# A planned order of work made anew: expert weight loads planned beside SyncE, other planned lengths for z's loads, stores and scatters

## The chip, the core and the metric

The kernel runs on one core of one Trainium2 chip. The core has a matrix engine (TensorE, here PE), a vector engine (VectorE, DVE), a scalar engine (ScalarE, ACT), a general engine (GpSimd, POOL) and an engine that issues DMA transfers (SyncE, SP). Each runs its own queue of instructions in order and meets the others through semaphores. The metric is the device time of one execution in microseconds; 876.67 us before the change (median of 3 runs, 876.44 to 877.49).

## What is computed

Four layers in a row, each followed by a residual add and a layernorm (float32, 8 sequences of 512 tokens, 256 features):

```python
x = _layernorm(x + _L0_attn_ref(x, ...))   # retention, 16 heads
x = _layernorm(x + _L0_ffn_ref(x, ...))    # ternary weights, GELU, layernorm inside
x = _layernorm(x + _L1_attn_ref(x, ...))   # per-token linear attention over the heads
x = _layernorm(x + _L1_ffn_ref(x, ...))    # mixture of experts, below
```

The change is mostly about the last layer. Tokens form two groups of 2048. Each group's tokens pick two of 8 experts (a capacity of 160 rows per expert and group); an expert is two matmuls with weights of 1 MB each, and its output, times the gate, is added back to the token's row:

```python
expert_in = jnp.einsum('gtec,gth->egch', dispatch, x)
h = jax.nn.relu(jnp.einsum('egch,ehf->egcf', expert_in, wi))
expert_out = jnp.einsum('egcf,efh->egch', h, wo)
y = jnp.einsum('gtec,egch->gth', combine, expert_out)
```

## The kernel before

The kernel is a set of streams of stages: per half or whole sequence `a0`, `a1`, `a2` (retention), `b`, `bn` (the ternary feed-forward), `c1`, `hd`, `ca`, `c2` (the second attention), then choosing and routing (`t`), loading expert weights (`w`, `load_expert`, line 1760), gathering rows (`g`, `gather`), transposing them (`d`), the two expert matmuls (`h`, `e`), adding back (`s`, `combine`, line 1904) and the last layernorm (`f`, `finish`, line 2071). Each stage is a Python generator.

No order stands in the code as such. While the kernel is built, a planner keeps a clock: `op` (line 204) books an instruction on an engine for a planned length (its `cost`) at the first gap after its inputs' planned times, and puts it into a heap by planned start; `flush` (line 277) emits instructions in that order. So planned times decide three things: the order of instructions in every engine's queue, which engine takes a copy (`either` picks the one that would be through first), and where PE gets fillers. They insert no wait: at run time an instruction waits for semaphores of its true dependencies, and behind what stands ahead of it in its queue.

`interleave` (line 343) takes the string `turns` (line 2189), one letter for each turn of a PE stage; the next turn goes to the first stage in the string that can open. Where the next stage opens more than 1.4 us of planned time after PE's planned clock, it emits fillers, matmuls on a constant into an unused bank (`spare`, line 403), one for each 0.44 us. A filler has no reader.

SP issues all plain transfers through `dma` (line 703): `cost` is the time that the planner keeps SP's line, 0.4 us where nothing else is said, plus 1.9 us until the data is there (`LAND`). An expert's two weight loads are planned with cost 5.0 each (2.5 for a half), so while a 1 MB load is under way no other transfer may stand on SP's planned line.

The expert layer in order: group 0 takes experts 0 to 7, group 1 experts 7 to 0. They are numbered 0 to 15 in that order. Three are kept in memory for both groups (8, 9 and 10 use the weights of 7, 6 and 5); 11 and 12 use other buffers; 13, 14 and 15 are loaded into the three slots that 8, 9 and 10 free (`wi_13`, `wo_13` and so on). The output of a pair of experts is `eoT`, 320 rows transposed; PE turns it back in three parts (`eo_tp`, line 1921), DVE or ACT multiplies it by the gate (`eo_g_c`, group and column c, three columns for a pair), and POOL adds it to the rows of y in DRAM by an indirect transfer (here a scatter). Scatters of a group write the same tensor, so each waits for the landing of the one before. `combine` plans that by `Plan.landed`: 2.5 us after the scatter's issue, or near the end of a weight load that SP's line shows at that time.

When a group's scatters have landed, `finish` loads y for a sequence (`z_b`, 512 KB, cost 2.4), makes its layernorm (statistics on DVE, a power on POOL, the product on DVE for group 0 and on ACT for group 1) and stores it (cost 2.0). z_0 to z_3 belong to group 0 and run beside group 1's experts; z_4 to z_7 come at the end. The last pair of experts is not scattered: its outputs are summed on PE (`tail_ps`) and go straight to the output rows, after all stores. The copy of the last `eoT` from the matmul's bank is on DVE.

Of the kernel before, what the change touches and what calls it, by code (L numbers as in the profile page):

```python
# [21 lines left out]
B, S, D = 8, 512, 256  # L22
# [6 lines left out]
G = 2  # L29
# [54 lines left out]
def tile_layers(ctx: ExitStack, tc: tile.TileContext, ins, out, at):  # L84
    nc = tc.nc
# [38 lines left out]
    y_d = [dram.tile([TG + P, D], F32, name=f"y_d{g}") for g in range(G)]  # L124
# [16 lines left out]
    ACT, DVE, POOL, SP, GELU, EXP, DVS, POOLD = range(8)  # L141
# [5 lines left out]
    LAND = 1.9  # L147
# [8 lines left out]
    class Plan:  # L156
        now = 0.0
        slow = 0.0
        t = 0.0
# [4 lines left out]
        loaded = None  # L164
        shared = None, -9.0
        landed = 0.0
        free = {
            k: [(0.0, i) for i in range(n)] for k, n in dict(
                m4=M4, aq=AQ, x=XB, T=TB, b8=B8, w=EW, xsT=2, eoT=2, hT=2, ex=EX, scm=SCM, qz=2,
# [516 lines left out]
    with ExitStack() as stages:  # L686
# [16 lines left out]
        def dma(t, out, in_, cost=0.4):  # L703

            return op(SP, cost, t, nc.sync.dma_start, out=out, in_=in_) + LAND

        def rows_x(b):
            return x_d[b].rearrange("(c p) d -> p c d", p=P)
# [1051 lines left out]
        def load_expert(i):  # L1760
            _, e = order[i]
            kept = i - 2 * (i - E) - 1 if i >= E else None
            t = Plan.t
            if kept is not None and kept >= E - EW:
                weights[i] = weights[kept]
            else:
                if i == spare_w[0]:
                    held = [slot_tile(wk, "b8", [P, 2, FF], f"w_{i}_{j}") for j in range(2)]
                    parts = [w[:, j] for w in held for j in range(2)]
                elif i == spare_w[1]:  # L1770
                    held = [
                        slot_tile(wk, tag, [P, FF], f"w_{i}_{tag}_{j}") for tag in ("T", "hh")
                        for j in range(2)
                    ]
                    parts = list(held)
                else:
                    held = claimed("w")[1]
                    pool = pools[0 if held < 2 else 1]
                    wi = pool.tile([P, NK, FF], F32, tag=f"wi{held}", bufs=1, name=f"wi_{i}")
                    wo = pool.tile([P, NK, FF], F32, tag=f"wo{held}", bufs=1, name=f"wo_{i}")  # L1780
                    parts = [w[:, j] for w in (wi, wo) for j in range(2)]
                from_wi = ins["L1_ffn_wi"][e].rearrange("(k p) f -> p k f", p=P)
                from_wo = ins["L1_ffn_wo"][e].rearrange("(j f p) d -> p j f d", p=P, j=2)
                if i in spare_w[1:]:
                    for j in range(2):
                        t = max(t, dma(Plan.t, parts[j], from_wi[:, j], cost=2.5))
                    for j in range(2):
                        to = parts[2 + j].rearrange("p (f d) -> p f d", d=D)
                        t = max(t, dma(Plan.t, to, from_wo[:, j], cost=2.5))
                else:  # L1790
                    whole = held if i == spare_w[0] else (wi, wo)
                    t = max(t, dma(Plan.t, whole[0], from_wi, cost=5.0))
                    to = whole[1].rearrange("p j (f d) -> p j f d", d=D)
                    to, got = (v.rearrange("p j f d -> p (j f) d") for v in (to, from_wo))
                    t = max(t, dma(Plan.t, to, got, cost=5.0))
                parts[2:] = [w.rearrange("p (f d) -> p f d", d=D) for w in parts[2:]]
                weights[i] = parts, held
            yield later(t)
            return t
# [104 lines left out]
        def combine(i):  # L1904


            g, e = order[i]
            last = i >= len(order) - 2
            pair, half = divmod(e, 2)
            n_in = added[g, pair]  # L1910
            for j in ((0, 1), (1, 2))[half]:
                n_in[j] += 1
            for j, n in enumerate(COLS):
                if n_in[j] != (1, 2, 1)[j]:
                    continue
                n_in[j] = -9
                col = pair * 3 + j
                yield from need(0.0)
                ps = bank("eo_tp")
                for m in range(NK):  # L1920
                    T.transpose(
                        ps[:n, m * P : (m + 1) * P], eoT[g, pair][:, m, j * P : j * P + n], ident
                    )
# [15 lines left out]
                Plan.landed = done + 2.5  # L1939
                for a, b in Plan.busy[SP]:  # L1940
                    if b - a > 2.2 and a < done + 1.5 and b > done:
                        Plan.landed = max(Plan.landed, b - 0.5)
                give(eo, Plan.landed)
            if max(n_in) < 0:
                give(xsT[g, pair], Plan.now)
                give(eoT[g, pair], Plan.now)
            yield later(done)
            return done + (0.0 if last else 2.9)
# [122 lines left out]
        def finish(b):  # L2071

            g = b * G // B
            z = slot_tile(wk, "x", [P, NC, D], f"z_{b}")
            t = Plan.t
            landing = dma(t, z, rows_of(y_d, b), cost=2.4)
            landing = max(landing, t + (9.0 if g == 0 else 4.0 + 2.9 * (b - B // G)))
            yield later(landing)
            while b > B - 3 and "shown" not in tail:
                yield later(Plan.t + 0.3)  # L2080
            if b > B - 3:
                landing = max(landing, tail["shown"])
            e = max(layernorm(wk, z, z, [landing] * NC, on_act=(g == 1)))

            def store():
                stored.append(
                    nc.sync.dma_start(out=out[b].rearrange("(c p) d -> p c d", p=P), in_=z)
                )

            e = op(SP, 2.0, e, store)  # L2090
            tail["stored"] = max(tail.get("stored", 0.0), e + 0.5)
            give(z, e + 2.0)
            yield later(e + 2.0)
            return e + 0.5

        def after(*keys):
# [90 lines left out]
            ],  # L2187
        }
        turns = (
            "llnnnnlbbbbbhbbelbnbleceeeebleeeeleebcbblellbbelbelllcllbcnclerebbblbeeebellelcnnnnl"  # L2190
            "nnbclnbnbnclnbcbrcbrnllbnlbllnnhhblnncllhhhhblnnclbbbcnnhnbhcbncnnblbbjnjlllnbnlbjln"
            "jjbbbjjbbcjbhlnjjhlnhjhhhljhlnjbhnhllnblffcfnnnjjcflllnjcjjnnbclblfljnbjbllnbjlbcjbj"
            "nnllbbnlcjnffcjnnnbclllhffchbbnnnnlhllnnnnflhlbbbnlbnblfflhfflhbbbnlljhhhflffblbllfl"
            "lfnlnnlcffnfjnjjjfhbbnncnbfjnjhcfnjjfhnnnlhhhjjncjcjnfbbhhhnbnbfllbjlhlnhlhnffnnflhh"
            "hjnfnjnncfhjcjjcnnjlnffchcjjnfhllfjlnnjnnjjfffnffnnlhnjhjhhhhhhfffhjjjnnnnfcfcncjjfn"
            "nffnccfnnfnhnffjjnnnjjnjfjfjhhhhnjjnhnhjnjhhjffofjmffnnnnfhjjfffjnnjjoffjffoohfhooho"
            "hhhjjoohjojjfffhjrfmfmffffjfffjjmfrqqrfjmjrmqjmrqmmrrqrqqjjjmfmffqfjfjffffrmqqjqjqrf"
            "fqfqfqfpqqqpqrrpprprqrrfrqfqfffqppffffqrpqrrrfqfqfrrffrprqqpqqzpqqqpmoprrrroomrmpmmo"
            "mromropomqoooqmqrrprqrqrqqqqqqqqqprprrrpqprrppqqrpqpqqqrpqqqqqprrqqqqqqqqqqqqqqqqqpq"
            "mrrppqprrmrrpppmrrrrrpprrqprpyzzzzppp"  # L2200
        )

        interleave(
# [33 lines left out]
```

## Time and profile before

| | |
|---|---|
| median of 3 runs | 876.67 us |
| the profiled execution | 876.54 us |
| its span, first to last instruction | 874.8 us |
| mean granted PE clock | 0.987 |
| DVE, ACT, POOL busy | 616.6, 516.2, 328.6 us |
| DVE busy from 600 to 650 us | 46.9 of 50 |
| transfers | 106.89 MB, 122 GB/s on the mean |
| SP's queue of transfers | 42.0% of the 16 engines' span |
| POOL's queue of transfers | 3.5% |
| weight loads wi, wo | 11 and 11 of 1024 KB, and one more expert in parts |
| z loads and stores | 8 and 8 of 512 KB |

The page gives busy time of each engine, then groups of instructions by line. Nearly all instructions but PE's carry line 233, where the planner stores them, so groups are told apart by their tiles (`eo`, `z`, `spare`). A line of a timeline has the start, the length, the engine, the line and the operation, and in brackets how long the engine had been idle and what ended it. Matmuls in float32 run as two passes, and a timeline counts passes.

### The profile page before, as it was taken

The page shows a single profiled execution, that of the slowest core. Times are in us where ns is not written, and L with a number is a line of the kernel's source. Part 1 is how long each engine was busy: PE and PEld are TensorE (multiplying, and loading weights), DVE is VectorE, ACT ScalarE, POOL GpSimd, SP SyncE. Part 2 cuts the span into 40 slices and gives each one's busy share as a digit, 9 for nine tenths or more (in the row PEclk, how much of TensorE's full clock was granted, in tenths as well). Part 3 has the DMA queues.
Part 4 walks back from the last instruction along what each step waited for, and adds up shares of the span by engine and source line. Part 5 has one row for each costly group of instructions (what it writes and reads, how often), then busy time and mean ns, then how long its engine had stood idle before and what let it go on. Part 6 is the DMA issues. An engine that isn't in the chain of part 4 may idle for free. (4 is left out here: it accounts for less than half of the span.)

```text
span 874.8 us, 20560 instructions
## 1 busy us (share of the span) xinstructions
PE 829.8 (95%) x8128; PEld 682.0 (78%) x8128; DVE 616.6 (70%) x1669; ACT 516.2 (59%) x1047; POOL 328.6 (38%) x346
## 2 busy tenths in 40 slices
PE   7998999999999999999999999999999999999983
PEld 5877877986878887688778768768578889889971
DVE  4946678587898888677878888899986553713324
ACT  2436568648673777568788597676755463222223
POOL 1222462352344442244353524425253231372433
PEclk9999999999999999999999999999999999999995
DMA  7153111652722033622515607566587195649553
GB/s 215 25 171 114 44 37 25 121 161 36 174 66 62 18 74 58 168 70 39 115 59 98 170 26 147 192 143 147 173 165 231 46 307 157 209 120 331 139 127 111
DMA packets 201615, 106.89 MB, mean 122 GB/s; under 512 B 124432, under 2 KB 192208, under 8 KB 201328
## 3 DMA queue, kind: packets, MB, share of 16 engines
q1 hardware_dynamic: 197664, 100.01, 42.0%
q0 software_dynamic: 3856, 5.57, 3.5%
q8 instruction: 64, 1.05, 0.5%
q14 instruction: 31, 0.25, 0.1%
HBM read 70.96 MB, written 30.41 MB: 116 GB/s over the span
## 5 line engine op out<-in xcount | busy, mean ns | idle before, releaser
L233 POOL TENSOR_TENSOR fsq<-fsq,fh 128x256 f32<-128x256 f32 x96 | 71.0, 739 | 59.3 <-ACT fh L233 34.0
L233 DVE TENSOR_TENSOR scm<-sc,cst 128x512 f32<-128x512 f32 x108 | 68.3, 683 | 13.8 <-PE sc L1138 13.6
L233 DVE TENSOR_TENSOR hm<-hs,cst 128x512 f32<-128x512 f32 x109 | 69.3, 682 | 10.8 <-PE hs L1592 10.7
L1368 PE MATMUL fc_ps<-x1T,fcT 128*128 128x256 f32 x512 | 71.6, 291 | 4.0 <-DVE x1T L233 3.5
L233 DVE SCALAR_TENSOR_TENSOR fT<-fh,lnf,fT 128x256 fp32r<-128x256 f32 x128 | 62.5, 536 | 15.6 <-ACT fT L233 15.1
L1368 PEld LDWEIGHTS fc_ps<-x1T,fcT 128*128 128x128 f32 x512 | 64.1, 191 | 8.1 <-DVE x1T L233 4.4
L1409 PE MATMUL pr_ps<-prT,fT 128*128 128x258 f32 x512 | 69.5, 290 | 0.0
L1409 PEld LDWEIGHTS pr_ps<-prT,fT 128*128 128x128 f32 x512 | 63.9, 189 | 3.4 <-issue 1.8
L1879 PE MATMUL wo_ps<-e_hT,wo 128*128 128x160 f32 x448 | 66.5, 301 | 0.0
L1065 PE MATMUL qk_ps<-xT,wqkv 128*128 128x256 f32 x256 | 62.4, 396 | 3.4 <-ACT xT L233 1.8
L1851 PE MATMUL wi_ps<-xsT,wi 128*128 128x160 f32 x448 | 64.9, 301 | 0.0
L233 POOL DMA_INDIRECT y_d<-eo,srci x21 | 33.1, 1574 | 82.8 <-DVE eo L233 30.3
L1879 PEld LDWEIGHTS wo_ps<-e_hT,wo 128*128 128x128 f32 x448 | 62.1, 190 | 1.6 <-issue 0.9
L1851 PEld LDWEIGHTS wi_ps<-xsT,wi 128*128 128x128 f32 x448 | 61.7, 190 | 1.1 <-ACT xsT L233 0.5
L233 ACT ACTIVATE fT<-fh,lnf 128x256 fp32r<-128x256 f32 x128 | 58.3, 499 | 1.7
L1500 PE MATMUL qk_ps<-x2T,l1T 128*128 128x512 f32 x128 | 58.5, 600 | 0.7 <-ACT x2T L233 0.7
L1065 PEld LDWEIGHTS qk_ps<-xT,wqkv 128*128 128x128 f32 x256 | 49.1, 197 | 12.4 <-ACT xT L233 4.7
L233 POOL TENSOR_TENSOR ln<-ln,mhalf 128x4 f32<-128x4 f32 x32 | 33.4, 1042 | 59.8 <-DVE ln L233 53.7
L233 ACT ACTIVATE e_hT<-wi_ps 128x480 f32<-128x480 f32 (+1 forms) x48 | 24.5, 522 | 48.6 <-PE wi_ps L1851 47.6
L233 POOL TENSOR_TENSOR scm<-scm,cst 128x512 f32<-128x512 f32 x20 | 25.6, 1283 | 70.7 <-ACT scm L233 30.3
L403 PE MATMUL spare<-cst,cst_ident 128*128 128x256 f32 x192 | 46.1, 384 | 0.0
L233 ACT ACTIVATE fh<-fh 128x512 f32<-128x512 f32 x64 | 39.6, 627 | 10.6 <-DVE fT L233 9.2
(283 smaller groups left out, 1947.2 us busy)
## 6 DMA issues: line engine op xcount, KB each, us to landing
wi<-in_L_ffn_wi SPq DMA_DIRECT2D x11, 1024.0 KB
wo<-in_L_ffn_wo SPq DMA_DIRECT2D x11, 1024.0 KB
hh<-k_d SPq DMA_DIRECT2D x32, 256.0 KB
hh<-q_d SPq DMA_DIRECT2D x32, 256.0 KB
xh<-in_L_attn_x SPq DMA_DIRECT2D x16, 256.0 KB
x<-in_L_attn_x SPq DMA_DIRECT2D x8, 512.0 KB
k_d<-qk SPq DMA_DIRECT2D x32, 128.0 KB
q_d<-qk SPq DMA_DIRECT2D x16, 256.0 KB
```

The lines of the kernel that those rows point to most:

```text
L233: heapq.heappush(Plan.events, (t, Plan.count, shares, t + cost, lambda: fn(*args, **kw)))
L403: T.matmul(ps[:, :256], ident, cst[:, :256], start=True, stop=True)
L1065: T.matmul(ps[:, m * HT : (m + 1) * HT], wqkv[:, k, which * D + m * P : which * D + (m + 1) * P], xT[:, k, :], start=(k == 0), stop=(k == ...
L1368: T.matmul(ps[:, j * HT : (j + 1) * HT], fcT[:, k, f * P : (f + 1) * P], x[:, k, :], start=(k == 0 and x is low), stop=(k == NK - 1 and x ...
L1409: T.matmul(acc[:, : D + 2], hs[:, part, f, c * P : (c + 1) * P], prT[:, f, :], start=(f == 0 and part == 1), stop=(f == NF - 1 and part == 0),
L1500: T.matmul(ps, l1T[:, k, which, m * P : (m + 1) * P], x2T[:, k, :], start=(k == 0), stop=(k == NK - 1),)
L1851: T.matmul(ps[:, f * CAP : (f + 1) * CAP], wi[k][:, (f3 + f) * P : (f3 + f + 1) * P], x[:, k, es], start=(k == 0), stop=(k == NK - 1),)
L1879: T.matmul(ps[:, m * CAP : (m + 1) * CAP], parts[2 + f // 4][:, f % 4, m * P : (m + 1) * P], hT[:, f, :], start=(f == 0), stop=(f == NF - 1),)
```

## The change

Weight loads get a helper of their own. It books SP for 1.0 us and plans the transfer itself on a line `Plan.wire` that only weight loads use, 5.0 us long (2.5 for a half), one after another. Their intervals are kept in `Plan.loads`:

```diff
+        wire = 0.0
+        loads = []
...
+        def load(t, out, in_, length=5.0):
+
+            begun = max(op(SP, 1.0, t, nc.sync.dma_start, out=out, in_=in_), Plan.wire)
+            Plan.wire = begun + length
+            Plan.loads.append((begun, Plan.wire))
+            return Plan.wire + LAND
...
-                        t = max(t, dma(Plan.t, parts[j], from_wi[:, j], cost=2.5))
+                        t = max(t, load(Plan.t, parts[j], from_wi[:, j], 2.5))
...
-                    t = max(t, dma(Plan.t, whole[0], from_wi, cost=5.0))
+                    t = max(t, load(Plan.t, whole[0], from_wi))
```

A scatter's planned landing looks at these intervals: beside a load it is 1.0 us after the load's planned end, though at most 7.0 us after the scatter's issue. The loads of z are planned at 0.55 us of SP's line instead of 2.4 and their landing in group 1 at 4.2 us and 1.0 more for each further sequence (before 4.0 and 2.9); the stores at 0.5 instead of 2.0, with 1.5 us added behind:

```diff
                 Plan.landed = done + 2.5
-                for a, b in Plan.busy[SP]:
-                    if b - a > 2.2 and a < done + 1.5 and b > done:
-                        Plan.landed = max(Plan.landed, b - 0.5)
+                for a, b in Plan.loads:
+                    if a < done + 1.5 and b > done:
+                        Plan.landed = max(Plan.landed, min(b + 1.0, done + 7.0))
...
-            landing = dma(t, z, rows_of(y_d, b), cost=2.4)
-            landing = max(landing, t + (9.0 if g == 0 else 4.0 + 2.9 * (b - B // G)))
+            landing = dma(t, z, rows_of(y_d, b), cost=0.55)
+            landing = max(landing, t + (9.0 if g == 0 else 4.2 + 1.0 * (b - B // G)))
...
-            e = op(SP, 2.0, e, store)
+            e = op(SP, 0.5, e, store) + 1.5
```

The string `turns` is another one from its first letters on (11 lines of letters, of which the first is shown), so stages take PE in another order from the start of the kernel:

```diff
-            "llnnnnlbbbbbhbbelbnbleceeeebleeeeleebcbblellbbelbelllcllbcnclerebbblbeeebellelcnnnnl"
+            "nlnnnllbbnbbrbbbnbbellheeebeleeeecelebebelllbbbbleelllbclclleeccbbblebeeelllbenncnnl"
```

In the instructions as built, this comes to the following. PE has the same matmuls and transposes but for the fillers, of which there are 83 instead of 96 (166 passes instead of 192). Locally, stages stand before or after others that were their neighbours. On SP, in the part that the prediction speaks of:

```
before: wi_13 wo_13 out<-z_0 out<-z_2 wi_14 wo_14 z_1 z_3 wi_15 wo_15 out<-z_1 out<-z_3 z_4 ...
after:  wi_13 wo_13 out<-z_0 out<-z_2 z_1 wi_14 wo_14 z_3 out<-z_1 wi_15 wo_15 out<-z_3 z_4 ...
```

Also on SP, the stores of x3 and y for sequence 3 stand behind wi_0 and wo_0 instead of before them, hh_5_3 (operands of the second attention) behind wi_1 and wo_1, and wi_4 ahead of the stores for sequence 6. On POOL the scatter of eo_1_11 stands ahead of the powers for z_0 and z_2 instead of behind them, and the order of scatters is the same (eo_1_11, 9, 10, 8, 6, 7, 5, 3, 4 for group 1). The power for z_1 stands behind the scatter of eo_1_10 and before that of eo_1_8 in the new order, behind eo_1_8 in the old one. On PE the parts eo_1_9 and eo_1_10 are turned back together, expert 10's wo and expert 12's wi change places with their neighbours, and eo_1_6 and eo_1_7 come inside and after expert 12's wo instead of before expert 12's wo. 18 copies and products that had been on ACT (with POOL for some) are on DVE and as many the other way round, among them eo_0_6, eo_1_8 and eo_1_10 (now ACT) and eo_1_6 and eo_1_7 (now DVE).

More of the change, by code (lines that the diff above doesn't have):

```diff
@@ L1785, in load_expert @@
                     for j in range(2):
-                        t = max(t, dma(Plan.t, parts[j], from_wi[:, j], cost=2.5))
+                        t = max(t, load(Plan.t, parts[j], from_wi[:, j], 2.5))
                     for j in range(2):
                         to = parts[2 + j].rearrange("p (f d) -> p f d", d=D)
-                        t = max(t, dma(Plan.t, to, from_wo[:, j], cost=2.5))
+                        t = max(t, load(Plan.t, to, from_wo[:, j], 2.5))
                 else:
                     whole = held if i == spare_w[0] else (wi, wo)
-                    t = max(t, dma(Plan.t, whole[0], from_wi, cost=5.0))
+                    t = max(t, load(Plan.t, whole[0], from_wi))
                     to = whole[1].rearrange("p j (f d) -> p j f d", d=D)
                     to, got = (v.rearrange("p j f d -> p (j f) d") for v in (to, from_wo))
-                    t = max(t, dma(Plan.t, to, got, cost=5.0))
+                    t = max(t, load(Plan.t, to, got))
                 parts[2:] = [w.rearrange("p (f d) -> p f d", d=D) for w in parts[2:]]
@@ L2189, in tile_layers @@
         turns = (
-            "llnnnnlbbbbbhbbelbnbleceeeebleeeeleebcbblellbbelbelllcllbcnclerebbblbeeebellelcnnnnl"
[L2191 to L2200, printed above, removed]
+            "nlnnnllbbnbbrbbbnbbellheeebeleeeecelebebelllbbbbleelllbclclleeccbbblebeeelllbenncnnl"
+            "nnblcnnbbnclncnbnbbcllbblllnnnlchhlbnhhlhhjnnblblbcbncnhnhcbbncnnblbbnjlllnnlnlbjbjj"
+            "bbbjjjhblbjjnhnhljhhhjlhbclbjnnhhlnlbrrlcfffnnncjlfljlbjjncjlnlncjblnbfjlblbjlcnjbnz"
+            "bjbllnbjnljcnffhcnnlfbnflblhcbnhnnnlllnnclnnlhblbbnnlfffbblhfflnhbblbjlhhhflflfllflc"
+            "lfnlnnnnlcbjfjfjjbfnfnbbnnhbjljncnffqfhhjnjnhhhjjcnjbjbcfnnnhjhhbbflbllhllhnnhffnnlj"
+            "hfhnhnjfcnfnhcjjjcnnlnqffchcjfjnjhllfjlnnnnjjjfffnffnlnnhjjhhhhhhhjffjfhjnnnnfcfcnjc"
+            "fmjnnffnccfnnmnhnfffjnjnnjjnffjjjmhjhhjhnnnjnhhfjhjhfjofffnnnnjffffjnjnffjjfohfojohf"
+            "hoohohhhojjohjjojfffhjffffffrjfffjjrfrfrjmrmpjqrrrmjqmqjjmqmqmjfffqffjjffffrqjqjqqrp"
+            "ffqfmmqqpfqfqqrprrqprqrprrqpffqfffpqrffffrpqqrrqffqffrrrfqqpqrqqqopprqrrrpoqoorrpooq"
+            "opoooprrrrrmpqqqmqqpppmmmmpqrqqpqrrrmqqqmrqrmrqprqqrpprrrqrqqqppqqqqqqqppqqpqrqqqqrr"
+            "rqqqqqqqqmmpppqqrrrmrrrprrppppzpzpzzy"
         )
```

## The prediction

> **What bounds the kernel now.** I read first the page's busy times, then the waits of TensorE (PE), then the timeline where PE waits longest.
>
> ```profile
> PE 829.8 (95%) x8128; PEld 682.0 (78%) x8128; DVE 616.6 (70%) x1669; ACT 516.2 (59%) x1047; POOL 328.6 (38%) x346
> L403 PE MATMUL spare<-cst,cst_ident 128*128 128x256 f32 x192 | 46.1, 384 | 0.0
> ```
>
> PE is busy for 829.8 of 874.8 us, but 46.1 of that is `spare`: fillers that the planner emits where its order leaves PE idle. There are 96 (two passes each), so one costs 46.1 / 96 = 0.48 us. Up to the last experts, then, time is PE's real work plus fillers plus short waits. Of the waits of PE, two concern the end:
>
> ```profile
> PE eo_tp L1921 <- DVE eoT L233: 5.1, 1, 5.1
> PE xs_tp L1827 <- DMA rows<-x_d,srci: 1.4, 2, 0.7
> ```
>
> The 5.1 us are the tail. VectorE (DVE) has the copy of `eoT` queued behind the statistics of z_4 and z_5:
>
> ```profile
> 842.48 2.02 SPq L233 DMA_DIRECT2D z<-y_d  x4
> 846.52 0.43 DVE L474 BATCH_NORM_STATS2 ln<-z 128x6 f32<-128x256 f32 x1 [16.53 <-DMA z<-y_d]
> 853.42 0.49 DVE L233 COPY eoT<-wo_ps 128x320 f32<-128x320 f32 x1
> 853.96 1.11 PE L1921 MATMUL eo_tp<-cst_ident,eoT 128*128 128x128 f32 x4 [5.09 <-DVE eoT L233]
> ```
>
> The z loads go out at 842.48, when the last scatter-add into y_d has landed; the chain of waits has that scatter from 838.62 for 3.84 us as its first piece. So the end (874.8 − 842.5 = 32.3 us later) hangs on a chain of nine scatters on GpSimd (POOL), one waiting for the landing of the one before. Six of them, and the DMA traffic of these stretches (columns: five busy times, clock, DMA share, GB/s):
>
> ```profile
> 794.61 1.50 POOL L233 DMA_INDIRECT y_d<-eo,srci  x1 [1.33 <-ACT eo L233]
> 802.76 1.60 POOL L233 DMA_INDIRECT y_d<-eo,srci  x1 [6.65 <-issue]
> 812.04 1.56 POOL L233 DMA_INDIRECT y_d<-eo,srci  x1 [7.68 <-DVE eo L233]
> 816.61 1.43 POOL L233 DMA_INDIRECT y_d<-eo,srci  x1 [3.00 <-issue]
> ...
> 834.04 1.55 POOL L233 DMA_INDIRECT y_d<-eo,srci  x1 [2.51 <-issue]
> 838.62 1.56 POOL L233 DMA_INDIRECT y_d<-eo,srci  x1 [3.02 <-DMA y_d<-eo,srci]
> ```
>
> ```profile
> 795.00:804.00 9.00, 9.00 (x70) 9.00 (x68) 0.48 (x1) 2.08 (x5) 2.35 (x2) 1.00 0.98 308
> 804.00:813.00 9.00, 9.00 (x66) 8.51 (x65) 1.90 (x7) 2.13 (x5) 1.32 (x2) 1.00 1.08 358
> 813.00:822.00 9.00, 9.00 (x68) 8.76 (x67) 4.79 (x19) 3.05 (x7) 4.56 (x5) 1.00 0.30 55
> ```
>
> The first two take 8.15 and 9.28 us each, beside 1 MB weight loads that fill the DMA engines (share 0.98 and 1.08). The line at 812.04 names a DVE copy as releaser, but that one (eo_1_8) only happened to end then; the rows this scatter sends (eo_1_10) were ready at 804.55, so it was the landing that it waited for. From 812.04 to 838.62 six steps take 26.6 us, 4.43 each. These two are what puts the chain behind PE: the last two `eo` are ready at 830.0 and 830.1, yet their scatters start at 834.04 and 838.62.
>
> **The change part by part.** No arithmetic changes. The two programs hold the same PE matmuls but for fillers, 83 for 96; SyncE (SP) issues the same 350 transfers; 18 PSUM copies and products change from DVE to ACT and as many back, POOL has one product fewer. All the rest is order.
>
> *Fillers*, by their groups in the trace:
>
> ```profile
> 354.50 1.03 PE L403 MATMUL spare<-cst,cst_ident 128*128 128x256 f32 x4
> 355.85 0.29 PE L1186 MATMUL r_ps<-q,state 128*64 128x128 f32 x1 [0.32 <-ACT qk L233]
> ...
> 360.90 3.19 PE L403 MATMUL spare<-cst,cst_ident 128*128 128x256 f32 x14
> 364.02 1.24 PE L1592 MATMUL hs<-hh 16*128 16x128 f32 x32
> ```
>
> Both groups go. The first covered a wait for the retention state, with 0.32 left over; now the scores sc_6_2 and a transpose (1.15 + 0.3 us of PE) stand there. The second covered the load of hs_2_0's operand, issued at 360.48 and so some 3.5 us long; now the second half of w1, sc_6_3, the transposes of x_4 and r_ps_6_2 (1.9 + 1.15 + 0.6 + 1.5 = 5.1 us) stand before hs_2_0. Real work instead of filler: −1.03 − 0.32 − 3.19 = −4.5. The group at 426.19 shrinks from 4 to 2 (−0.95, matmul behind it ready at once; half, −0.5). The one at 549.86 shrinks from 6 to 3 (−1.42), but PE then waits 0.79 more for `a` from ACT, so the wait returns: 0. The one at 766.20 goes from 4 to 3 and its place is before the transposes of rows_1_3, for which PE waited 1.4 longer: their gathers stand on POOL behind a chained scatter. In the new order eo_0_6 is scaled on ACT; in the old one its scatter started at 753.85, released by DVE's routing, so it and those behind it can start earlier: 0 to −1.9, I take −0.9. Two single fillers and one group of 3 come in and one of 8 becomes 5: +0.48 × 2 + 1.4 − 1.4 = +1.0, half of which I take as waits of the old order: +0.5. Sum −5.4. The other waits in the answer on PE's waits, without the start and the tail, sum to some 19 us and belong to the old order; a new one has others, and I allow 7% more, 1.4: **−4.0**. Ends: −6.2 (13 × 0.48, all fillers) and +1.4 (every wait returns, the allowance stays).
>
> *Scatter chain.* On SP z_1's load now precedes wi_14 and wo_14, and out<-z_1 precedes wi_15 and wo_15; on POOL eo_1_11 goes ahead of two powers. Positions on PE, from the first matmul of expert 8's wi (771.18), a block of 16 matmuls being 4.34 us (833.82 to 838.16), a pair of transposes 0.22: eo_1_9 and eo_1_10 come together after 100 matmuls (six blocks and four, 27.1 us) and 1.7 us of transposes, at 800.0, ready at about 801; counted on in the same way, eo_1_8 is ready at 810, eo_1_6 at 816.3, eo_1_7 at 818.7, the last two at 830 as before, since as many matmuls stand before them. Loads: z_1, wi_14, wo_14, z_3 follow out<-z_2 (issued 794.7) as before, 3.1 MB at 0.337 MB/us (the stretch from 783 to 795 moved 337 GB/s) until some 805.5. eo_1_9, out at 801, lands with them at 805.5; eo_1_10 goes at 805.5. Behind it on POOL stands the power of z_1's layernorm (1.05 us), behind that DVE's four products (1.38), then out<-z_1 and only then wi_15 and wo_15, at about 810. So eo_1_10 meets a lull and lands at 810 (4.43), eo_1_8 goes at 810 and is caught until those 2.6 MB are through, 818. Then 4.43 each: eo_1_6 818, eo_1_7 822.4, eo_1_5 826.9, eo_1_3 831.3, eo_1_4 835.7, landed at 839.6 instead of 842.5: **−2.9**. Ends: if none is caught, eo_1_3 goes at 830.1 as it is ready, landing at 838.4, −4.1; if the catch takes the whole 9.28, 840.9, −1.6.
>
> [...]
>
> *The tail after it* is unchanged in order but for one small DVE instruction of z_4 put one chunk later, in 0.7 us in which DVE waited for POOL anyway: 0 (at best −0.5). What stands before it on PE is done at 848.9, ahead of the copy of `eoT` at 853.42 − 2.9, so DVE still sets the end and all of the 2.9 arrives there.
>
> *Moves costed at nothing.* The stores of x3 and y for batch 3 fall behind wi_0 and wo_0; they are read at 640.29 (first gather), 85 us after their issue at 555.4; uncovered, 2.1 MB / 0.337 = 6.2 us. hh_5_3 falls behind wi_1 and wo_1; issued at 569.35, used at 592.8, cover 23 us against the same 6.2. wi_4 moves ahead of batch 6's stores; behind it wait those stores (in 695.5, read after 765). wi_15 at 810 is used at 838.
>
> **Sum.** −4.0 − 2.9 = −6.9: span 874.8 → 867.9. The profiled run took 876.54, 1.74 more than its span and 0.13 under the median 876.67. Against the median: **869.8 us**.
>
> **Rivals.** (1) *Fillers return as waits*: the dependency that each covered is late all the same. For: PE waits right after the groups at 354.50 and 549.86. Against: the largest is followed by more real work than the load takes. 876.7 − 2.9 = 873.8. (2) *The change doesn't do what it says*: planned lengths move nothing in hardware and the chain ends where it did. For: loads and scatters are the same bytes on the same engines, and one scatter is still caught. 876.7 − 4.0 = 872.7. (3) *Both*: 876.7. (4) *Slower: more scatters caught behind loads.* With wi_15 later, loads are spread over a longer time. Each further one caught costs 9.28 − 4.43 = 4.85 us. With two beyond mine the last lands at 839.6 + 9.7 = 849.3, +6.8 against before; less 4.0 is +2.8: 879.5. With one it is 839.6 + 4.85 = 844.4, +1.9 − 4.0, still faster; it decides from the second. Against: the two bursts last some 10 and 8 us, room for two catches in all.
>
> **How the numbers follow.** Mine 0.50 (866.5 to 872.5), rival 1 0.15, rival 2 0.13, rival 3 0.13, rival 4 0.09. A measurement of this kernel tells about 0.2%, 1.75 us, from no change. Faster: mine and rivals 1 and 2, 0.78; same 0.13; slower 0.09. Lower end: all fillers and no catch, −6.2 − 4.1 = −10.3, 866.4, less 1.4 for waits of PE that shrink too: 865. Upper end: rival 3's middle, 876.2; beyond lie rival 4 and half of rival 3, 0.15, and some 0.04 below.
>
> **What would show it.** Right: PE's `spare` at 166 passes; no PE wait of 3 us at hs_2_0; the gaps between scatters of eo_1_9, eo_1_10, eo_1_8 about 4.5, 4.4 and 8; the z loads 2.9 us earlier after expert 8's first matmul; the gap at `eo_tp` near 2.2. Wrong: PE's waits grown by what the fillers lost, or three gaps over 8 us in the chain.

## The result and the profile after

The kernel after takes 880.95 us (median of 11 runs), the kernel before 877.88 beside it. The ratio on record is 1.0047 (95% interval 1.0032 to 1.0062; that of the two medians is 1.0035). It is slower by 3 to 4 us, where 869.8 us and a gain were forecast. The profiled execution has a span of 878.9 us against 874.8.

First the fillers, in the page's busy times and then in the groups by line (busy us and mean ns behind the bar):

```profile
PE 826.9 (94%) x8102; PEld 678.1 (77%) x8102; DVE 616.8 (70%) x1669; ACT 516.9 (59%) x1047; POOL 326.0 (37%) x345
```

```profile
L405 PE MATMUL spare<-cst,cst_ident 128*128 128x256 f32 x166 | 40.5, 386 | 0.0
```

They went as said: 166 passes, 40.5 us instead of 46.1. But PE is busy 2.9 us less in a span 4.1 us longer, so 7.0 us of waiting are new. The view of PE's waits (sum in us, times, longest) has the largest two, the first of them forecast at 2.2:

```profile
PE eo_tp L1930 <- DVE eoT L235: 6.1, 1, 6.1
PE tp L462 <- DVE a L235: 5.1, 2, 4.3
```

The place of a loss is found by following the same instruction through both traces (us from the span's start), here the last transpose of the logits of a sequence (`lg_tp`) and then the z loads of group 1:

| | before | after | difference |
|---|---|---|---|
| logits of sequence 6 | 700.9 | 696.5 | −4.4 |
| logits of sequence 7 | 736.6 | 738.6 | +2.0 |
| first z load of group 1 | 842.5 | 847.1 | +4.6 |
| end of the span | 874.8 | 878.9 | +4.1 |

So the forecast gain was there at 697 us. Between the two logits 6.4 us were lost, and from there to the z loads 2.6. Now the first loss. `a_7` is the attention result of sequence 7; an RMS norm scales it before PE transposes it, and `rms_ss` holds that norm's sums and then their power. Rows of all engines of the kernel after:

```profile
703.35 1.59 POOL L235 DMA_INDIRECT y_d<-eo,srci  x1 [9.49 <-ACT xsT L235]
705.69 0.17 DVE L235 TENSOR_SCALAR rms_ss<-rms_ss 128x4 f32<-128x4 f32 x1
710.38 1.43 POOL L235 DMA_INDIRECT y_d<-eo,srci  x1 [5.44 <-issue]
711.34 1.54 POOL L235 TENSOR_TENSOR rms_ss<-rms_ss,mhalf 128x4 f32<-128x4 f32 x1
712.91 1.70 ACT L235 ACTIVATE t<-g3b,rms_ss 128x256 f32<-128x256 f32 x4 [5.29 <-POOL rms_ss L235]
714.65 1.23 DVE L235 TENSOR_TENSOR a<-a,t 128x1024 f32<-128x1024 f32 x1 [8.45 <-ACT t L235]
716.02 1.94 PE L462 MATMUL tp<-cst_ident,a 128*128 128x128 f32 x8 [4.30 <-DVE a L235]
717.75 2.34 PE L1888 MATMUL wo_ps<-e_hT,wo 128*128 128x160 f32 x8
```

Read it from the bottom: PE waits 4.30 us for the transposes of a_7, DVE waited 8.45 for ACT's four products, ACT 5.29 for the power `rms_ss` on POOL. The operand of that power was ready at 705.86. It ran at 711.34 because the scatter of eo_0_2 stands ahead of it in POOL's queue and waits there for the landing of the scatter of 703.35, which took 7.0 us. In the old order the power stands ahead of that scatter, and PE waits 0.63 us (kernel before):

```profile
711.95 1.63 POOL L233 TENSOR_TENSOR rms_ss<-rms_ss,mhalf 128x4 f32<-128x4 f32 x1
717.76 1.50 POOL L233 DMA_INDIRECT y_d<-eo,srci  x1 [4.18 <-DVE choose L553]
716.73 1.06 PE L460 MATMUL tp<-cst_ident,a 128*128 128x128 f32 x8 [0.63 <-DVE a L233]
```

The waiting engine is named DVE, the missing one is POOL, and what it waits for is a transfer whose result the power doesn't need.

What follows runs slower too. Two windows of the kernel after (the columns are us, five busy times, granted clock, DMA share, GB/s):

```profile
712.00:716.00 4.00, 0.00 (x0) 0.01 (x1) 1.23 (x1) 3.06 (x6) 0.88 (x1) 0.84 0.19 31
716.00:720.00 4.00, 3.98 (x17) 4.00 (x18) 2.04 (x8) 3.52 (x7) 1.95 (x2) 0.50 0.02 4
```

After the wait the clock is 0.50 (1.00 from 716 to 720 us in the kernel before), and the eight transposes take 1.94 us instead of 1.06 in the kernel before. In single microseconds of the kernel after, with PE idle from 711.72, it is 1.00 up to 714 us, 0.87 in the next and 0.50 from 715 to 721.

The second loss, in the tail (two rows of DVE, then POOL's scatters of eo_1_9, 10, 8, 6, 7 and the last one, eo_1_4):

```profile
791.02 0.47 DVE L235 TENSOR_SCALAR eo<-eo_tp,sgate 64x256 f32<-64x256 f32 x1 [19.60 <-PE eo_tp L1930]
791.42 0.41 DVE L476 BATCH_NORM_STATS2 ln<-z 128x6 f32<-128x256 f32 x1
804.51 1.61 POOL L235 DMA_INDIRECT y_d<-eo,srci  x1 [5.69 <-DVE eo L235]
812.02 1.55 POOL L235 DMA_INDIRECT y_d<-eo,srci  x1 [5.89 <-issue]
816.56 1.48 POOL L235 DMA_INDIRECT y_d<-eo,srci  x1 [1.91 <-issue]
824.30 1.61 POOL L235 DMA_INDIRECT y_d<-eo,srci  x1 [4.71 <-DMA y_d<-eo,srci]
829.27 1.55 POOL L235 DMA_INDIRECT y_d<-eo,srci  x1 [3.36 <-issue]
...
842.15 1.55 POOL L235 DMA_INDIRECT y_d<-eo,srci  x1 [2.92 <-ACT eoT L235]
```

The steps are 7.51, 4.54, 7.74 and 4.97 us: two slow ones where one was forecast and one stood before (9.28, 4.57, 3.95, 5.02). The first two lines are a wait of the same kind as the first loss: the product for eo_1_11, now on DVE, waits for PE until 791.02, with the statistics of z_0 behind it, whose load was issued at 782.98. In the kernel before, that load was issued at 781.53, and the statistics waited for nothing but its landing:

```profile
785.85 0.43 DVE L474 BATCH_NORM_STATS2 ln<-z 128x6 f32<-128x256 f32 x1 [17.02 <-DMA z<-y_d]
```

### The profile page after: what moved, and what is told of

Read it like the earlier page. It is cut to its first block, busy times and chain, and to the rows that moved or that the text cites. A ratio compares the mean times of both kernels' runs of the same rounds, so it can differ in the third digit from the quotient of the medians.

```text
span 878.9 us, 20512 instructions
## 1 busy us (share of the span) xinstructions
PE 826.9 (94%) x8102; PEld 678.1 (77%) x8102; DVE 616.8 (70%) x1669; ACT 516.9 (59%) x1047; POOL 326.0 (37%) x345
## 5 line engine op out<-in xcount | busy, mean ns | idle before, releaser
L235 DVE SCALAR_TENSOR_TENSOR fT<-fh,lnf,fT 128x256 fp32r<-128x256 f32 x128 | 60.4, 520 | 10.1 <-ACT fT L235 9.7
L1860 PEld LDWEIGHTS wi_ps<-xsT,wi 128*128 128x128 f32 x448 | 61.8, 190 | 0.9 <-issue 0.4
L235 ACT ACTIVATE fh<-fh 128x512 f32<-128x512 f32 x64 | 39.7, 628 | 9.7 <-DVE fT L235 8.7
L235 ACT ACTIVATE x<-x,ln 128x256 f32<-128x256 f32 x64 | 33.2, 590 | 18.8 <-DVE ln L235 18.8
```

Source lines behind the costliest of these rows:

```text
L235: heapq.heappush(Plan.events, (t, Plan.count, shares, t + cost, lambda: fn(*args, **kw)))
L1860: T.matmul(ps[:, f * CAP : (f + 1) * CAP], wi[k][:, (f3 + f) * P : (f3 + f + 1) * P], x[:, k, es], start=(k == 0), stop=(k == NK - 1),)
```

## The experiments

Most edits change one place in one engine's queue and leave planned times and all other queues alone. `marks(name, fn)` notes that an instruction has been emitted; `behind(name, fn)` holds one back until then. Ratios are to the kernel before, run beside.

**The power ahead of the scatter, on the kernel after** (a_power_first).

```diff
+                scatter = GP.indirect_dma_start
+                if (g, col) == (0, 2):
+                    scatter = behind(("power", 7), scatter)
...
-                    POOLD, 1.58, max(t, Plan.landed), GP.indirect_dma_start,
+                    POOLD, 1.58, max(t, Plan.landed), scatter,
...
-            e = rsqrt(rs, rs, 1.0 / D, RMS_EPS, e)
+            e = rsqrt(rs, rs, 1.0 / D, RMS_EPS, e, wrap=lambda fn: marks(("power", b), fn))
```

> The kernel after, with one POOL instruction moved: the scatter-add of eo_0_2 is emitted behind the power of batch 7's RMS instead of ahead of it; planned times, and the order on every other engine, stay. Main theory (the power stands behind a scatter that waits 7.0 us for the landing of the scatter before it, so a_7 comes 4.3 us late and TensorE then runs some 10 us at a lower clock): the power runs at about 706 instead of 711.3, the wait of 4.30 us ahead of the transposes of a_7 falls under 1 us, the eight transposes take 1.04 us instead of 1.94 and the eight matmuls of w_ps 3.6 instead of 4.4, the logits of batch 7 come 7 us earlier (731.6 instead of 738.6), and the whole time falls by 5 to 7 us: 0.992 to 0.994 of the kernel after, 0.996 to 0.999 of the kernel before. Rival 1 (the tail's chain of scatters sets the end whatever happens here): the logits come 7 us earlier, the end less than 2.5 us. Rival 2 (a_7 is late because VectorE or ScalarE is late, not POOL): the wait at the transposes stays over 3 us and the time changes by less than 1 us.

Measured: 0.9994 (0.9972 to 1.0015) against 1.0047 for the kernel after, a little above the range given. Its timeline:

```profile
705.38 1.79 POOL L235 DMA_INDIRECT y_d<-eo,srci  x1 [9.29 <-ACT xsT L235]
708.24 1.06 POOL L442 TENSOR_TENSOR rms_ss<-rms_ss,mhalf 128x4 f32<-128x4 f32 x1 [1.07 <-DVE choose L559]
711.81 2.25 POOL L435 DMA_INDIRECT y_d<-eo,srci  x1 [2.51 <-DMA y_d<-eo,srci]
713.78 1.04 PE L483 MATMUL tp<-cst_ident,a 128*128 128x128 f32 x8
715.75 3.60 PE L1715 MATMUL w_ps<-aT,l1T 128*128 128x512 f32 x8
```

No wait, 1.04 us for the transposes. From the logits of sequence 6 to those of 7 it takes 34.9 us, after 42.1, before 35.6: the power's place costs 7.2 us there, and 0.53% of the time, 4.6 us. Rival 2 falls. Rival 1 allows less than 2.5 us at the end, and taken together the two intervals reach down to about 2.4; two more pairs below that differ only by this move (a_eo11_act and p_eo11_act, a_all_tail and p_all_tail), 0.82% and 0.65% apart, speak against it.

**The reverse on the kernel before** (b_power_behind, then b_power_behind2). In the first form the power was emitted late, behind ScalarE's four products that need it, so that kernel computes something else; in the second the scatter was emitted early (`pulled` holds the scatter of eo_0_2, `first` names it for sequence 7 alone):

```diff
+        def power_of(*args):
+            if first:
+                pulled[first]()
+            return GP.tensor_tensor(*args)
```

> The kernel before, with the reverse done to it: the power of batch 7's RMS is emitted behind the scatter-add of eo_0_2, nothing else. Main theory: in the kernel before this scatter runs at 717.76, so the power goes from 711.95 to between 716 and 719, a_7 comes 4 to 7 us later, TensorE waits 4.5 to 7.5 us ahead of its transposes (0.63 before) and runs slower after that; the whole time grows by 5 to 9.5 us, 1.006 to 1.011 of the kernel before. Rival (the place of the power on POOL is harmless; the kernel after loses elsewhere): within 1.5 us of the kernel before.

> The kernel before with the reverse edit: the scatter-add of eo_0_2 is emitted right ahead of the power of batch 7's RMS instead of right behind it; nothing else moves. (In the first form of this run the power was emitted late instead, behind ScalarE's four scalings that read its result: they read the sum of squares before its power there.) Main theory: the power waits behind the scatter for the landing of the scatter before (5.9 us after it in the first form), TensorE waits 4 to 7.5 us ahead of the transposes of a_7 (0.63 in the kernel before), and the whole time is 1.005 to 1.011 of the kernel before. Rival (this place on POOL is harmless; the kernel after loses elsewhere): 0.998 to 1.002.

Measured: 1.0091 (1.0067 to 1.0114) and 1.0109 (1.0090 to 1.0128). The second:

```profile
710.67 1.57 POOL L1955 DMA_INDIRECT y_d<-eo,srci  x1 [7.01 <-ACT rms_sq L233]
718.17 1.44 POOL L1955 DMA_INDIRECT y_d<-eo,srci  x1 [5.94 <-issue]
719.13 1.55 POOL L448 TENSOR_TENSOR rms_ss<-rms_ss,mhalf 128x4 f32<-128x4 f32 x1
723.83 1.94 PE L478 MATMUL tp<-cst_ident,a 128*128 128x128 f32 x8 [8.00 <-DVE a L233]
```

A wait of 8.00 us, 0.5 over the range given, and the logits of sequence 7 9.7 us later. With the run above, this settles the first loss: made in one kernel, unmade in the other.

**The load beside the scatter held back, on the kernel after** (a_load_later).

```diff
+                if behind_scatter:
+                    tc.add_manual_dep(
+                        made.ins, emitted["scatter", 0, 1].ins.name,
...
-                    t = max(t, load(Plan.t, whole[0], from_wi))
+                    t = max(t, load(Plan.t, whole[0], from_wi, behind_scatter=i == 6))
```

> The kernel after, with the load of expert 6's wi (1 MB, issued at 701.43) made to wait until the scatter-add of eo_0_1 (703.35) has landed; orders on all engines stay. If it is this load that keeps the scatter from landing for 7 us: the scatter lands in 4 to 4.6 us, that of eo_0_2 and the power behind it come 2.4 to 3 us earlier, the wait at the transposes of a_7 falls from 4.30 to 1.3 to 1.9 us, the clock holds, and the end is 3 to 5.5 us earlier than in the kernel after. If the landing is slow for another reason (the chain itself, the rows): the gap between the two scatters stays near 7 us and the time does not fall.

Measured: 1.0011 (0.9993 to 1.0029).

```profile
705.34 1.57 POOL L442 DMA_INDIRECT y_d<-eo,srci  x1 [9.62 <-ACT xsT L235]
709.83 1.43 POOL L442 DMA_INDIRECT y_d<-eo,srci  x1 [2.91 <-issue]
715.48 1.06 PE L483 MATMUL tp<-cst_ident,a 128*128 128x128 f32 x8 [1.89 <-DVE a L235]
```

The same scatter lands in 4.49 us instead of 7.0, the wait is 1.89. So it is the 1 MB load that makes the landing late (expert 6's wo stands behind it on SP and moved with it), and without it beside the scatter the kernel after gains 0.36%, some 3 us.

**Fillers put into the wait, on the kernel after** (a_warm; `warm` is 8 for a_7 and 0 elsewhere).

```diff
+            if k == 0:
+                for _ in range(warm):
+                    T.matmul(ps[:, :256], ident, cst[:, :256], start=True, stop=True)
```

> The kernel after, with eight more filler matmuls (some 3.8 us) put on TensorE right ahead of the transposes of a_7, into the wait of 4.30 us. They cannot shorten the wait, only keep TensorE busy in it. If the idle time itself lowers the clock of what follows: the wait is filled, the eight transposes take about 1.04 us instead of 1.94, the eight matmuls of wo_ps 1.25 instead of 2.34, those of w_ps 3.6 instead of 4.4, and the end comes 2 to 2.8 us earlier than in the kernel after (0.997). If the slower matmuls have another cause (the transfers, the operands): no change from the kernel after within 0.7 us, or 0.3 us slower.

Measured: 1.0049 (1.0031 to 1.0068), against 1.0047 for the kernel after and not 0.3% below it, as was expected.

```profile
712.14 3.62 PE L463 MATMUL tp<-cst,cst_ident 128*128 128x256 f32 x16
716.66 1.09 PE L465 MATMUL tp<-cst_ident,a 128*128 128x128 f32 x8 [0.90 <-DVE a L235]
717.59 1.25 PE L1891 MATMUL wo_ps<-e_hT,wo 128*128 128x160 f32 x8
```

The instructions behind it are faster (1.09 and 1.25 us instead of 1.94 and 2.34), the clock from 700 to 750 us is 1.00 instead of 0.93, and it takes 39.9 us between the two logits instead of 42.1, so the idle time did lower the clock. That 2.2 us did not show in the time, whose interval is some 3 us wide; that part stays inconclusive.

**The tail: does the chain of scatters set the end?** (p_scatter_less, on a_power_first: the scatter of eo_1_6 is left out, so 128 rows are missing in the sum.)

```diff
+                if (g, col) == (1, 6):
+                    scatter = lambda **kw: None
```

> The kernel after with the power ahead of the scatter, and without the scatter-add of eo_1_6 (128 rows of group 1 are not added into y), one link of the chain of nine. If the chain of scatters sets the end: the z loads of group 1 go out 4.4 to 7 us earlier and the end comes 4 to 7 us earlier than with the power first alone, 0.991 to 0.996 of the kernel before. If TensorE sets the end (its last matmuls before the tail are done at 846.3 there, with 6.6 us of waiting behind them): the z loads come earlier, the end less than 2 us.

Measured: 0.9939 (0.9921 to 0.9956), 4.8 us under a_power_first; the z loads 102.7 us after the logits of sequence 7 instead of 108.3. It does.

**The tail's moves, one by one and together.** On a_power_first: expert 15's loads ahead of the store of z_1 (p_wi15_early); eo_1_11 on ACT (p_eo11_act; alone on the kernel after, a_eo11_act); that and its scatter behind the powers of z_0 and z_2 (p_eo11_pool); that and the loads (p_eo11_wi15); all (p_all_tail; without the power's move, a_all_tail).

```diff
-            e = op(SP, 0.5, e, store) + 1.5
+            e = op(SP, 0.5, e, behind("wo_15", store) if b == 1 else store) + 1.5
...
-                t = either(pe(0.24), (ACT, ...), (DVE, ...), bank=ps, use=eo)
+                t = either(pe(0.24), *ways[: 1 if (g, col) == (1, 11) else 2], bank=ps, use=eo)
...
+                if (g, col) == (1, 11):
+                    scatter = behind(("z", 2), scatter)
```

> The kernel after with the power ahead of the scatter (as run before), and one move of the change undone in the tail: on SP the loads of expert 15's wi and wo go ahead of the store of z_1, as in the kernel before. Theory (the tail's chain did not get shorter because these 2 MB, issued late, slow two further scatters, eo_1_8 to eo_1_6 7.9 us and eo_1_6 to eo_1_7 6.1 us, beside the one slowed already, eo_1_9 to eo_1_10 7.8 us): the loads come some 9 to 11 us earlier, eo_1_9 to eo_1_10 grows to 8 to 9.5 us, the two others fall to 4 to 5 us, the z loads start 70.5 to 72 us after the first matmul of expert 8 instead of 74.1, and the end is 2 to 3.5 us earlier than with the power first alone: 0.995 to 0.998 of the kernel before. Rival (the chain follows TensorE's eo, not the loads): the gaps change place but the z loads stay within 1 us of 74.1, and so does the end.

> The kernel after with one instruction given back to the engine that the kernel before has it on: the scaling of eo_1_11 by its gates goes from VectorE to ScalarE. In the kernel after it stands on VectorE ahead of the statistics of z_0 and waits there for TensorE until 791.02, some 4 us after z_0 has landed. Theory (this wait holds the layernorms of z_0 and z_2, so their stores, and behind these on SP the loads of z_1 and of experts 14 and 15, which then meet the chain of scatters later): the statistics of z_0 start as z_0 lands, 3 to 4 us earlier, the load of expert 14's wi is issued 2.5 to 4 us earlier against the logits of batch 7 (62.7 us after them in the kernel after, 58.6 in the kernel before), the z loads of group 1 come 2 to 5 us earlier against the same logits (108.5 in the kernel after, 105.9 in the kernel before), and the end 2 to 5 us earlier than in the kernel after: 0.999 to 1.003 of the kernel before. Rival (as many bytes meet as many scatters, whenever they start): z loads and end within 1.5 us of the kernel after.

> Both single edits on the kernel after: the power of batch 7's RMS ahead of the scatter-add of eo_0_2 on POOL, and eo_1_11 scaled on ScalarE. If the two losses are separate, their gains add: 7 to 10 us under the kernel after, 0.994 to 0.997 of the kernel before, with the wait ahead of a_7's transposes under 1 us and the z loads of group 1 at 103.5 to 106.5 us after the logits of batch 7 (108.3 with the power alone). Rival (one bound behind the other): no more than 1.5 us better than with the power alone (0.998 to 1.000).

> The kernel with both edits, and a third place of the same kind: on POOL the scatter-add of eo_1_11 goes behind the powers of z_0 and z_2 (as in the kernel before), instead of ahead of them. Theory: those powers come 2 to 3 us earlier, the stores of z_0 and z_2 and the load of expert 14's wi 2 to 3 us earlier than with both edits alone, and the end 0 to 2.5 us earlier (the scatter has 12 us to the next of the chain, so that its delay costs nothing). Rival: the loads come earlier and catch as many scatters: no change within 1 us.

> The kernel with both edits, and the loads of expert 15 ahead of the store of z_1 on SP, as in the kernel before. The move alone changed which steps of the chain are slow (eo_1_10 to eo_1_8 7.9 us instead of eo_1_8 to eo_1_6) and not the sum. With all loads some 3 us earlier they can be through before eo_1_8: one step under 5 us more, and the end 1 to 4 us earlier than with both edits alone. If the sum of slow steps is what the bytes make it: within 1 us of both edits alone.

> The kernel after with the power first, and all three tail moves undone together: eo_1_11 scaled on ScalarE, its scatter-add behind the powers of z_0 and z_2, the loads of expert 15 ahead of the store of z_1. If the spread of the loads makes the chain slow: expert 14's wi is issued some 58.3 us after the logits of batch 7 and expert 15's 2 to 4 us after z_3's load, all of them are through by some 74, eo_1_9 goes at 64.3 and is slowed once (7.5 to 9.5 us), the steps behind it take 4 to 5.5 us each (at most one more of 6), the sum from eo_1_9 to the z loads falls from 42.7 to 39.5 to 41, the z loads come at 104 to 105.5 instead of 107.1 to 108.3, and the end is 1.5 to 3.5 us earlier than in any of the forms before: 0.9935 to 0.997 of the kernel before. Rival: the sum stays at 42 to 43.5, z loads at 106.5 to 108, time 0.998 to 0.999 as in the two forms with both edits.

> The kernel after with the three tail moves undone together and the power left behind the scatter. If the two losses are separate: the wait of 4.30 us ahead of a_7's transposes stays (3.8 to 4.8 us, the transposes at 1.94), and the z loads come at 104 to 106 us after the logits of batch 7 instead of 108.5, so that the end is 2 to 4 us earlier than in the kernel after, 1.000 to 1.003 of the kernel before. If only the power matters: 1.004 to 1.006, like the kernel after.

Measured, in us: from the logits of sequence 6 to those of 7, from the scatter of eo_1_9 to the z loads, and from the logits of 7 to the load of wi_14 and to the z loads. The distances in a row are from one profile of that kernel, the ratio is from all its runs:

| | 6 to 7 | eo_1_9 to z | wi_14 | z | ratio to before, interval |
|---|---|---|---|---|---|
| before | 35.6 | 39.7 | 58.6 | 105.9 | |
| after | 42.1 | 42.6 | 62.7 | 108.6 | 1.0047, 1.0032 to 1.0062 |
| a_power_first | 34.9 | 43.1 | 62.0 | 108.3 | 0.9994, 0.9972 to 1.0015 |
| p_wi15_early | 34.9 | 42.7 | 61.8 | 107.1 | 0.9984, 0.9967 to 1.0002 |
| a_eo11_act | 40.9 | 43.7 | 61.0 | 108.2 | 1.0061, 1.0042 to 1.0080 |
| p_eo11_act | 34.9 | 42.6 | 60.9 | 107.2 | 0.9979, 0.9962 to 0.9996 |
| p_eo11_pool | 34.9 | 42.8 | 58.3 | 107.1 | 0.9992, 0.9975 to 1.0009 |
| p_eo11_wi15 | 34.9 | 42.6 | 60.6 | 106.8 | 0.9978, 0.9962 to 0.9993 |
| p_all_tail | 34.9 | 40.4 | 58.3 | 104.9 | 0.9961, 0.9943 to 0.9979 |
| a_all_tail | 41.0 | 40.1 | 58.7 | 104.6 | 1.0026, 1.0005 to 1.0046 |

Each move alone, or two, fell short of what I expected: the loads came earlier and the chain was slowed at other steps, 42.6 to 43.7 us in sum. All three together nearly gave the old sum back (40.4 and 40.1, before 39.7). The scatters of p_all_tail (eo_1_9, 10, 8, 6, 7):

```profile
797.81 1.59 POOL L235 DMA_INDIRECT y_d<-eo,srci  x1 [6.83 <-DVE eo L235]
806.85 1.56 POOL L235 DMA_INDIRECT y_d<-eo,srci  x1 [7.46 <-ACT eo L235]
812.33 1.47 POOL L235 DMA_INDIRECT y_d<-eo,srci  x1 [2.84 <-issue]
816.98 1.60 POOL L235 DMA_INDIRECT y_d<-eo,srci  x1 [2.10 <-DVE eo L235]
821.56 1.55 POOL L235 DMA_INDIRECT y_d<-eo,srci  x1 [2.98 <-DVE eo L235]
```

One step of 9.04 us, then 5.48, 4.65 and 4.58. wi_15 was issued at 795.70 and wo_15 at 801.70; the DMA share is 1.09 from 799 to 808 us and 0.51 from 808 to 817 (1.14 from 809 to 810 and 0.22 from 810 to 811), so the loads were through some 3 us after eo_1_10 went out and 2 us before eo_1_8 did. In a_all_tail the wait for a_7 stays (4.27 us) and the tail is mended, 1.0026: the two losses are separate. p_all_tail is faster than both kernels.

**The wait ahead of the last eo_tp** (p_tail_act on a_power_first: the last copy of eoT on ACT; p_copy_first on p_all_tail: z_4 and z_5 planned not before that copy).

```diff
+            if i == 2 * E - 1:
+                done = op(ACT, 0.46, t, A.copy, to, got, bank=ps)
...
-            while b > B - 3 and "shown" not in tail:
+            while b > B - 5 and "shown" not in tail:
...
-            if b > B - 3:
+            if b > B - 5:
```

> The kernel after with the power ahead of the scatter, and the last copy of eoT moved from VectorE, where it stands behind the statistics of z_4 and z_5, to ScalarE, which is idle then. The wait of TensorE of 6.6 us ahead of the last eo_tp shrinks to under 1 us. If that wait is on the path that sets the end: 3 to 5 us earlier than with the power first alone. If the end hangs on the z loads, VectorE's statistics and the stores behind them: the wait goes and the end moves by less than 1 us (VectorE is free of the copy's 0.49 us).

> The kernel with the power first and all three tail moves undone, and the layernorms of z_4 and z_5 planned not before the last copy of eoT (as those of z_6 and z_7 are already): the copy goes to ScalarE ahead of the products of z_4. The wait of 3.82 us ahead of the last eo_tp falls under 1 us. If that copy and TensorE's sums behind it set the end (21.3 us from the copy's start to the last instruction in four profiles): 2 to 4 us earlier than with the four edits. If the end hangs on the z loads, VectorE's statistics, the powers and the stores, as the chain of waits of that kernel shows: the distance from the z loads to the end (31.67 us there) changes by less than 1 us, and so does the time.

The first, 0.9996 (0.9979 to 1.0013), missed what it was for: on ACT the copy stood behind the products of z_4 and z_5, and the wait was 7.9 us. In the second, 0.9982 (0.9964 to 1.0000), it is gone:

```profile
843.75 0.66 PE L1952 MATMUL eo_tp<-cst_ident,eoT 128*128 128x128 f32 x4
843.76 0.43 DVE L497 BATCH_NORM_STATS2 ln<-z 128x6 f32<-128x256 f32 x1 [5.41 <-DMA z<-y_d]
```

The edit also put z_6's statistics first, whose load is issued third and took 7.1 us, so the distance from z loads to end, 35.5 instead of 31.7 us, is no fair measure. From the first statistics to the end it is 27.3 us; with the wait, 27.8 in p_all_tail and in the kernel after. The wait of 3.82 us went and 0.5 us came of it, so it is not this wait that sets the end. That the chain of statistics, powers, products and stores does is read from the chain of waits, not tested by itself.

## Why the prediction was wrong

*Fillers, −4.0: right in kind, and eaten away later.* No wait of 3 us at hs_2_0, and the logits of sequence 6 at −4.4. That profile was a good one, though: over 14 profiles of the new order and 3 of the old, the mean gain is 5.3 us at sequence 3, 3.1 at sequence 4 and 2.2 at sequence 6. The step from 3 to 4 shows in a window of the kernel after, against the same window of the kernel before:

```profile
605.00:612.00 7.00, 5.53 (x70) 3.83 (x68) 5.76 (x20) 3.83 (x7) 3.77 (x5) 0.78 0.62 191
```

```profile
605.00:612.00 7.00, 7.00 (x76) 6.41 (x74) 6.72 (x20) 2.75 (x6) 5.57 (x7) 1.00 0.57 185
```

In the new order the transposes of another `a` stand there one by one behind ACT's products, and the clock falls to 0.78. This is a mean: in single microseconds it is 1.00 up to 608, where PE was busy for 1.5 of the last 3 us, and 0.50 from 609 to 612. My allowance of 1.4 us for new waits had no clock in it. This is read from the windows; no run took it apart.

*"All the rest is order", and "moves costed at nothing": this step failed.* My list of moves on POOL had eo_1_11 and two powers, not the power of sequence 7 behind the scatter of eo_0_2. It alone costs 0.53% of the time (4.6 us; 0.65% and 0.82% in the two other pairs), more than the fillers gave. None of my rivals had it: rival 4 looked for the price of a late scatter in the chain of scatters, not in what stands behind it on POOL.

*Scatter chain, −2.9: wrong in sign.* The step "z_1, wi_14, wo_14, z_3 follow out<-z_2 (issued 794.7) as before" failed: z_1's load went out at 800.70, and wi_14's behind it 62.7 us after the logits of sequence 7 instead of 58.6, because eo_1_11 stood ahead of the statistics of z_0 on DVE and ahead of their power on POOL (undoing both, p_eo11_pool, gives 58.3). I had named the second of these moves and costed neither. So eo_1_9 met the loads at their start (7.51 us, not 4.5), and the late loads of expert 15 slowed eo_1_8 (7.74, the one catch that I had, at about the same length). From eo_1_9 to the z loads it took 42.6 us, not 38.6 (839.6 − 801). The chain also began late. The sum put eo_1_9 29.8 us behind expert 8's first matmul (801 − 771.18); it went out 31.8 us behind it (804.51 − 772.69). The sum of PE's work up to there held to 0.4 us; missing in it was a wait of PE for ACT's copy of eo_1_11's `eoT`:

```profile
772.69 8.17 PE L1860 MATMUL wi_ps<-xsT,wi 128*128 128x160 f32 x56
790.57 0.41 PE L1930 MATMUL eo_tp<-cst_ident,eoT 128*64 128x128 f32 x2 [1.45 <-ACT eoT L235]
```

So the z loads came 74.4 us after that matmul, where 68.4 was forecast and 71.3 stood before. Rival 4 had the price of one more catch about right (4.85 us against these 4.0), but with it alone the kernel was to stay faster. That the end follows the chain was right (p_scatter_less), and so was the tail's 0 (32.3 to 31.8 us from the z loads on). That "DVE still sets the end" through the copy of eoT does not fit p_copy_first: PE's wait for that copy went, and 0.5 us came of it.

*The change's own aim.* It plans a weight load on a line of its own and a scatter's landing by that line. Its planned times, as the code works them out while the kernel is built (no trace shows them), have wi_6 begin at 717.7, since both weight tiles of a slot are free to the planner only when the expert is through; on the chip SP issued it at 701.43, as the last matmul on the old wi ended. So the planner saw no load beside eo_0_1's scatter, planned its landing 2.5 us after its issue was to end (701.75 + 2.5 = 704.25), and put the scatter of eo_0_2 there, ahead of a power that it planned to end at 709.0. In the old plan this scatter was to go at 715.1, behind the power, which was to end at 713.7.

## What to carry to other kernels

In an in-order queue, ask of every instruction with a far wait (a landing, another engine) what stands behind it, and whether that is on the critical chain: here a power of 1.54 us behind a scatter cost more (4.6 us) than 13 fillers gave (2.2 us at sequence 6, on the mean of the profiles). When an order is made anew, compare each engine's queue around its waiting instructions, not only what the change is about. Where bursts of loads meet a chain of dependent small transfers, count how many links they touch: here undoing one or two causes moved the slow link, and only all three together removed it.

## What the runs showed that was not expected

From a scatter to the next that waits for its landing it took 3.8 to 4.6 us in calm stretches and 7.0 to 9.3 where it went out amid 1 MB loads, whichever link it was (eo_0_1, eo_1_9, eo_1_10 and eo_1_8 each in some profile); some steps lay between, as the 4.97 us above. After a wait of 4.30 us PE's clock was 0.50, and with fillers in the wait it was 1.00 (a_warm, 700 to 750 us); it fell to 0.50 from 609 to 612 us as well, where no gap was longer than 0.99 us (the transposes at 606 us). The last transpose of sequence 6's logits began between 695.5 and 700.0 us in the 14 profiles of the new order, whose instructions are the same up to there: this point moves by 4.5 us from run to run, as much as the whole effect, so that distances between two anchors tell more than times.
